# GpSimd stands until a landing behind every four indirect transfers in a row instead of every six

## The chip, the cores and the metric

The kernel runs on one core of a Trainium2 chip. The number that counts is the device time of one execution in microseconds (us), as the median of the runs shown. A profile is one separate execution with the hardware profiler on; it has its own span and its own time.

The engines are named as in the profile: PE (TensorE matmul), PEld (its weight loads), DVE (VectorE), ACT (ScalarE), POOL (GpSimd), SP (SyncE, which here only issues plain transfers). A name with a q, such as SPq, is the engine's instruction queue.

## The reference, cut to what matters

The input is 32 sequences of 128 tokens with 128 features. Two layers follow, each a conditioning step and a mixture of experts, and each adds its result to `x`:

```
x = x + moe_attention(modulated_head_mixing(x, cond))     # layer 0
x = x + moe_ffn(conditioned_embedding(x, ids, states))    # layer 1

# layer 0: 16 experts, softmax over the experts whose gate is open, at least the two best
q, k, v = (sum_e w[n, e] * (h[n] @ proj[e]) for each of the three projections)
o       = softmax(q k^T / sqrt(128)) v                    # per sequence
out[n]  = sum_e w[n, e] * (o[n] @ o_proj[e])
# layer 1: 8 experts, the two best, weights from their logits
out[n]  = sum_e c[n, e] * (silu(h[n] @ gate[e]) * (h[n] @ up[e])) @ down[e]
```

What counts here is that a token goes to two experts. So a token's row has to be carried to the place of its expert and its result carried back.

## The kernel before, in words

**The sparse path.** The function `two_experts` does the work. (A second function, `every_expert_kernel`, stands behind a branch for inputs in which some token needs more than two experts, and is not run with these inputs.) Tokens are taken in four parts of eight tiles of 128 tokens in each layer. For a part, `front0` or `front1` computes the conditioned rows and the gates, and `route` works out for each token and each of its two experts a row number (`place` for the way there, `back` for the way back). Rows are then moved through DRAM, sorted by expert into blocks of 128 rows.

**Six kinds of indirect transfers.** They move 128 rows each, they are all issued by POOL, and there are 64 of each kind, 384 in all (`scatter` and `gather`):

- `rows_x`: the rows of layer 0 to their experts (scatter), before the q, k, v projections
- `gq`: the q, k, v rows back to the tokens (gather, 384 features), before the attention of one tile
- `rows_o`: the attention's rows to their experts (scatter)
- `ygo`: the output projection's rows back (gather), added to `X`
- `rows_c`: the rows of layer 1 to their experts (scatter)
- `ygc`: the rows of layer 1 back (gather), added to `X`, which goes to `out` afterwards

Between them SP moves whole blocks with plain transfers: `crx`, `cro` and `crc` read the sorted rows, `outs_x`, `outs_o` and `outs_c` write the experts' results. A read of a part's blocks waits for all of its scatters, and a gather waits for all of its results. The experts' matmuls are `qkv` and `yo` in layer 0 and `gu` (gate and up) and `yc` (down) in layer 1. The gather buffers are few: four of `gq`, three pairs of `yg`.

**The planner.** The kernel is not written in the order in which it runs. Class `Turns` records every operation as a node, with the time that it is expected to take and its dependencies, and `arrange` makes an order for all engines at once: `backward` gives due times, `forward` is a list schedule that keeps a clock for each engine, and the best of `ROUNDS` passes is taken. `trace` then emits the instructions in that order, and each engine runs its own list strictly in it. Since one helper emits them all, nearly every row of the profile has line L341.

**The rests.** `forward` counts POOL's transfers in a row. A transfer continues the run if it can begin less than `GAP` (1.2 us by the planner's clock) after the one before it. When the run has reached `RUN`, the planner lets POOL's clock pass by `REST` (1.6 us) and notes a rest before that transfer:

```
if not node.size or begin - free[name] >= self.GAP:
    run = 0
elif run == self.RUN:
    begin, run = free[name] + max(self.REST, begin - free[name]), 0
    rests.add(i)
run += 1 if node.size else 0
```

In the program a rest is a memset of eight columns of a tile `idle` that nobody reads (line L620). `trace` gives it, and it alone, a real wait on the instructions before it in POOL's list; for an indirect transfer that is its landing. If the instructions before it are scatters of one group, it waits for all of them. What comes after the memset on POOL stands behind it.

Of the kernel before, what the change touches and what calls it, by code (L numbers as in the profile page):

```python
# [110 lines left out]
class Turns:  # L111
# [20 lines left out]
        "POOL": {"rows_x": 1.45, "rows_o": 1.32, "gq": 1.29, "rows_c": 1.25, "ygo": 1.23, "ygc": 1.22},  # L132
    }
    TABLES = {AF.Exp: "exp", AF.Tanh: "tanh", AF.Silu: "silu"}
    RUN, REST, GAP = 6, 1.6, 1.2
    LOOK, HASTE = 0.8, 10.0
    HOP = 0.05
    READ_US, WRITE_US, ROWS_US = 1.7, 1.9, 1.2
# [2436 lines left out]
```

## Time and profile before

| | before |
|---|---|
| runs | 916.92, 911.39, 911.41 us; median 911.41 us |
| profiled execution, its own time | 922.13 us |
| its span, first to last instruction | 920.2 us |
| mean granted TensorE clock | 0.812 |
| busy share: PE, PEld, DVE, ACT, POOL | 66%, 45%, 55%, 45%, 44% |
| POOL: indirect transfers, rests | 384, 58 |
| DMA moved | 116.39 MB, 126 GB/s over the span |
| share of 16 DMA engines: SP's transfers, POOL's transfers | 30.1%, 12.4% |

The profiled execution took 1.2% more than the median of the runs, so differences are carried over rather than absolute times. A group's row gives line, engine, operation, output and inputs, count, busy time, mean of one in ns, and after the second bar the engine's idle time just before such instructions with what ended most of it. The busy time of a transfer on POOL is that of issuing it; its landing is seen only in who waits for it.

### The profile page before, as it was taken

How to read it: one execution, taken by the hardware profiler on the slowest of the kernel's cores; microseconds unless marked ns; L12 is line 12 of the kernel's file. 1: busy time of each engine (PE TensorE's matmuls, PEld its weight loads, DVE VectorE, ACT ScalarE, POOL GpSimd, SP SyncE). 2: the span in 40 equal slices, each digit the busy share in tenths (PEclk: the TensorE clock that was granted, in tenths of full speed). 3: DMA queues.
4: the chain of work that ended last, by engine and by line, in shares of the span. 5: the costliest groups of instructions: out<-in, count | busy, mean ns of one | idle time of the engine just before them, and what ended most of it. 6: DMA issues, size and time to landing. Idle time of an engine off the chain costs nothing.

```text
span 920.2 us, 10753 instructions
## 1 busy us (share of the span) xinstructions
PE 610.7 (66%) x2962; PEld 412.7 (45%) x2962; DVE 509.9 (55%) x1629; ACT 410.1 (45%) x1076; POOL 406.8 (44%) x457
## 2 busy tenths in 40 slices
PE   5167456975875686383676556767787878898830
PEld 3155335553553555251544344435464545665520
DVE  7988989687896460020465636534724765532311
ACT  3223342643654464271474246465453454453420
POOL 1000044056366664454555555455556562554424
PEclk9577577996998799596877578679998999797975
DMA  7980003421625578569733273431545214124221
GB/s 202 319 246 1 0 29 90 172 101 50 198 80 172 163 215 273 163 199 293 198 93 81 64 193 97 105 107 46 145 138 145 55 61 120 47 73 136 76 66 48
DMA packets 134043, 116.39 MB, mean 126 GB/s; under 512 B 9560, under 2 KB 121112, under 8 KB 133976
## 3 DMA queue, kind: packets, MB, share of 16 engines
q1 hardware_dynamic: 119640, 82.04, 30.1%
q0 software_dynamic: 14336, 33.58, 12.4%
q8 instruction: 28, 0.46, 0.2%
q14 instruction: 39, 0.32, 0.1%
HBM read 56.86 MB, written 58.72 MB: 126 GB/s over the span
## 4 chain that ended last, share of the span: by engine, by line
PE 32%; DMA 16%; issue 12%; POOL 9%; ACT 6%; DVE 5%; another core or an unknown queue 2%; POOLq 0%; SPq 0%; ACTq 0%; DVEq 0%
PE gu L341 7%; PE yc L341 4%; DMA gq<-outs_x,back 4%; DMA outs_x<-yx 3%; DMA ygo<-outs_o,back 3%; POOL rows_x L341 3%; PE qkv L341 3%; PE phT L341 2%; DMA rows_x<-h,place 2%; POOL gq L341 2%; PE yo L341 2%; PE pre L341 2%; PE pat L341 2%; PE pcrc L341 1%
## 5 line engine op out<-in xcount | busy, mean ns | idle before, releaser
L341 POOL DMA_INDIRECT rows_x<-h,place x64 | 79.3, 1240 | 187.8 <-DVE place L341 130.4
L341 PE MATMUL pat<-ident,prodv 128*128 128x128 f32 x512 | 79.3, 315 | 38.9 <-DVE prodv L341 18.1
L341 PE MATMUL gu<-w1e,crTc 128*128 x176 | 97.1, 650 | 3.5 <-DVE hh L341 2.6
L341 PE MATMUL qkv<-wq,crTx 128*128 x216 | 86.7, 524 | 9.6 <-ACT yx L341 7.5
L341 POOL DMA_INDIRECT ygc<-outs_c,back x64 | 60.8, 950 | 71.5 <-DMA outs_c<-ycs 45.1
L341 PEld LDWEIGHTS pat<-ident,prodv 128*128 128x128 f32 x512 | 68.9, 164 | 48.6 <-issue 25.2
L341 POOL DMA_INDIRECT gq<-outs_x,back x64 | 69.0, 1078 | 28.1 <-issue 18.6
L341 DVE TENSOR_TENSOR prodv<-S,kx 128x2048 f32<-128x2048 f32 x32 | 72.9, 2289 | 11.7 <-PE pat L341 11.3
L341 POOL DMA_INDIRECT rows_o<-orow,place x64 | 66.0, 1031 | 22.8 <-issue 17.0
L341 DVE TENSOR_TENSOR hh<-hh,gu 128x256 f32<-128x256 f32 x88 | 36.7, 418 | 68.8 <-ACT hh L341 52.3
L341 POOL DMA_INDIRECT rows_c<-crow,place x64 | 62.2, 973 | 25.0 <-issue 19.6
L620 POOL MEMSET idle<- 128x8 f32 x58 | 6.1, 104 | 147.2 <-DMA ygo<-outs_o,back 35.1
L341 POOL DMA_INDIRECT ygo<-outs_o,back x64 | 60.9, 952 | 22.4 <-issue 17.5
L341 ACT COPY yx<-qkv 128x384 f32<-128x384 f32 x108 | 50.5, 482 | 27.9 <-PE qkv L341 12.0
L341 PE MATMUL yc<-w1e,hT 128*128 x352 | 54.4, 296 | 11.7 <-ACT ycs L341 5.8
L341 DVE SCALAR_TENSOR_TENSOR X<-ygc,share,X 128x128 f32<-128x128 f32 x64 | 21.3, 348 | 71.3 <-DMA ygc<-outs_c,back 51.4
L341 PEld LDWEIGHTS yc<-w1e,hT 128*128 128x128 f32 x352 | 48.2, 206 | 23.5 <-ACT hT L341 11.2
L341 DVE SCALAR_TENSOR_TENSOR gq<-gq,w 128x384 f32<-128x384 f32 x32 | 19.5, 615 | 68.9 <-DMA gq<-outs_x,back 57.3
L341 ACT ACTIVATE hh<-gu 128x256 f32<-128x256 f32 x88 | 34.5, 392 | 51.7 <-PE phT L341 33.3
L341 PEld LDWEIGHTS qkv<-wq,crTx 128*128 128x128 f32 x216 | 38.6, 202 | 33.6 <-ACT yx L341 13.4
L341 DVE SCALAR_TENSOR_TENSOR X<-ygo,w,X 128x128 f32<-128x128 f32 x64 | 21.8, 344 | 52.4 <-DMA ygo<-outs_o,back 47.4
L341 DVE TENSOR_TENSOR prod<-kx 128x1152 f32<-128x1152 f32 x32 | 43.3, 1353 | 4.9 <-issue 1.8
(289 smaller groups left out, 1404.9 us busy)
## 6 DMA issues: line engine op xcount, KB each, us to landing
outs_x<-yx SPq DMA_DIRECT2D x24, 768.0 KB
crx<-rows_x SPq DMA_DIRECT2D x12, 512.0 KB
cro<-rows_o SPq DMA_DIRECT2D x12, 512.0 KB
outs_o<-yos SPq DMA_DIRECT2D x12, 512.0 KB
crc<-rows_c SPq DMA_DIRECT2D x8, 512.0 KB
outs_c<-ycs SPq DMA_DIRECT2D x8, 512.0 KB
rows_x<-zeros SPq DMA_DIRECT2D x2, 1728.0 KB
rows_o<-zeros SPq DMA_DIRECT2D x2, 1728.0 KB
```

The source lines that it names most:

```text
L341: node.give = lambda: getattr(real, op)(turns.real(out), *map(turns.real, args), **{k: turns.real(v) for k, v in kw.items()})
L620: tn.rest = lambda: nc.gpsimd.memset(idle, 0.0)
```

## The change

One constant of the planner is changed. A rest is put in when the run has reached four transfers instead of six. The rest itself, the planner's price for it (`REST`) and the gap that ends a run (`GAP`) stay as they were. The order of all engines is planned anew with it.

```
-    RUN, REST, GAP = 6, 1.6, 1.2
+    RUN, REST, GAP = 4, 1.6, 1.2
```

## The prediction

> **What bounds the kernel now.** I read the page's groups first, then POOL's timeline, then the table by stage, then the chain. In the groups (busy, mean ns | idle before and its releaser) POOL's rests stand out: the memset itself is 104 ns, but POOL is idle before it.
>
> ```profile
> L620 POOL MEMSET idle<- 128x8 f32 x58 | 6.1, 104 | 147.2 <-DMA ygo<-outs_o,back 35.1
> L341 POOL DMA_INDIRECT gq<-outs_x,back x64 | 69.0, 1078 | 28.1 <-issue 18.6
> ```
>
> That is 147.2 / 58 = 2.54 us of standing per rest. POOL's timeline (start, us, what, idle before) shows one rest in place, and a transfer issued after a long pause:
>
> ```profile
> 315.42 0.95 POOL L341 DMA_INDIRECT rows_o<-orow,place  x1 [0.30 <-issue]
> 318.18 0.11 POOL L620 MEMSET idle<- 128x8 f32 x1 [1.81 <-DMA rows_o<-orow,place]
> 318.85 0.96 POOL L341 DMA_INDIRECT rows_o<-orow,place  x1 [0.56 <-issue]
> ...
> 257.83 1.80 POOL L341 DMA_INDIRECT rows_x<-h,place  x1 [11.61 <-DVE place L341]
> ```
>
> Without a rest the next transfer begins 0.30 us after the last one ends. With it, it began at 318.85 after an end at 316.37: 2.48 us, so the rest costs 2.48 - 0.30 = 2.18 us there. I worked this out for all 58: mean 2.94 us, least 1.77, most 6.41.
>
> The table by stage (us, then PE, PEld, DVE, ACT and POOL busy with counts, PE clock, DMA share, GB/s):
>
> ```profile
> 188.00:258.00 70.00, 48.98 (x252) 34.33 (x250) 57.16 (x105) 34.68 (x95) 37.47 (x33) 0.83 0.33 102
> 258.00:348.00 90.00, 65.37 (x331) 45.22 (x331) 59.57 (x145) 48.67 (x141) 60.26 (x55) 0.89 0.53 173
> 348.00:600.00 252.00, 153.88 (x718) 105.35 (x716) 96.86 (x467) 115.76 (x282) 130.04 (x153) 0.75 0.54 158
> 600.00:888.00 288.00, 232.80 (x1157) 152.46 (x1157) 133.47 (x580) 138.57 (x371) 140.62 (x166) 0.91 0.33 94
> 888.00:920.20 32.20, 0.00 (x0) 0.00 (x0) 5.62 (x16) 0.00 (x0) 15.31 (x18) 0.50 0.18 50
> ```
>
> POOL's 44% busy hides the truth of 188 to 600. There it issues 208 transfers (224.4 us of busy time), with 208 x 0.30 = 62 us between them and 32 rests of 3.26 us each (104 us). Together that is 391 of 412 us. Only three pauses are no rest: 11.6, 5.3 and 2.1 us, together 18 us above the usual 0.30. So in this stretch POOL works without a break, and what it carries is waited for: over the whole run DVE stands 57.3 us for `gq` and 47.4 us for `ygo`. From 600 on PE is busy 81% of the stage and sets the pace; behind 888 there are only `ygc` gathers and their additions.
>
> The chain of waits says the same (start, us, what):
>
> ```profile
> 572.03 5.87 DMA rows_c<-crow,place
> ...
> 578.21 0.10 POOL idle L620
> 578.32 0.56 issue
> 578.88 0.96 POOL rows_c L341
> ```
>
> Here a rest is a link of the chain: landing, memset, next scatter. Counting such links from 188 to 600 gives 14 of the 32 rests, with a mean cost of 3.24 us; from 600 to 888 none of 22; behind 888 both.
>
> **The change part by part.** I listed POOL's queue as each program builds it. Before: 384 transfers, 58 rests. After: 384 transfers, 90 rests. By the transfers they stand behind: the first 16 (`rows_x` of part 0) 2 to 3; the next 208, which are 188 to 600, 32 to 50; the next 144, to 888, 22 to 34; the last 16 (`ygc` of part 3) 2 to 3. No transfer is added or taken away. SP issues the same plain transfers with few places swapped, while about a fifth of DVE's and ACT's lists differ in order. I price that at nothing, within plus or minus 5 us as an estimate: no stage or dependency is altered by it.
>
> *First 16 scatters, one more rest.* POOL starts them when `place` is ready (122.0) and SP's queue stands for their landing (`crx` goes out at 153.35). Behind the added rest is the remainder of the part, and all of it is on the path. The two rests there cost 1.77 and 3.18, mean **2.5 us**.
>
> *188 to 600, 18 more rests.* What is queued behind an added memset is every later gather and scatter, and for those wait DVE (`gq`, `ygo`), PE (attention) and SP (`crx`, `cro`, `crc`). Two bounds. From below: the share of rests that is on the chain stays 14 of 32, so 18 x 14/32 = 7.9 rests at 3.24 = 25.5 us. From above: POOL is never caught up, so all 18 x 3.26 = 59 us arrive at 600, or 41 us if the 18 us of pauses take up part. I take 25.5, since it is counted on the path, and keep 41 and 59 for the range. The covers of the other rests are PE and DVE work on the front of the next parts; if that cover goes, the sum moves to the upper bound. At the floor of 1.77 per rest the lower figure would be 14 us.
>
> *600 to 888, 12 more rests.* None of 22 is on the chain. POOL pauses here anyway, waiting for `outs_c`: 16.5 us at 780, 7.6 at 843 and 21.0 at 888, 45 us in all against 12 x 2.59 = 31 us of added standing. Hidden behind PE: **0**. Without that cover it is 31. The thin spot is 832, where the last scatter of part 3 ends as the read `crc` goes out on the chain.
>
> *The last 16 gathers, one more rest.* Nothing else runs. The two rests cost 2.42 and 2.08, mean **2.25 us**.
>
> *Does a shorter run make anything cheaper?* The Trainium skill, DMA: Bandwidth & Descriptors, section on the anatomy of a SWDGE DMA, puts some 2.0 us of fixed cost on such a transfer, most of it the receipt of the last write. Taken as the price of one wait (plus 64 KB / 436 GB/s = 0.15), it makes the 7.9 rests 17 us and the whole 22. The row says 3.24 per rest: up to 6.41 where the landing meets SP's writes. I go by the row. The other hope is that issuing itself gets faster with fewer transfers in flight: 33 us of the 384 transfers' busy time lie above 0.95 us each. By place in the run the mean excess is 0.08, 0.12, 0.07, 0.06, 0.08, 0.12 us from first to sixth, with no trend, and the transfer at 257.83 took 1.80 us after 11.6 us of standing. The skill's SBUF page (SBUF: two separate sides) has another reason, that some DVE operations lock GpSimd out while it writes descriptors; by stage the row fits it: mean 1.27 us from 188 to 348 where DVE is busy 73%, 0.97 behind 348 where it is 38%. By depth, dropping the fifth and sixth place would save some 3 us; by the lock nothing. I take nothing.
>
> **Sum:** 2.5 + 25.5 + 0 + 2.25 = +30 us. The profiled execution, 922.1, would become 952. Carried to the median of the runs, 911.4 + 30 = **942 us**, 3.3% slower.
>
> **The rivals.** About 1% (9 us) is what a measurement of this kernel can tell from no change.
>
> *POOL alone is the bound (0.25).* All added rests up to 600 arrive at the hand-over to layer 1's experts, whose first blocks wait for `rows_c` of part 0 (last scatter at 583.9). For: the account of 391 of 412 us. Against: half the chain there is PE, DVE or SP. 41 + 4.75 = 46 gives 957; without the pauses 59 + 4.75 = 64 gives 975.
>
> *Only the ends pay (0.13).* The added rests in the middle fall where the chain is elsewhere, or the new order starts gathers early enough. For: 18 of 32 rests there were off the chain. Against: DVE's waits for gathers. 2.5 + 2.25 gives 916.
>
> *Less crowding pays (0.05), faster.* Fewer transfers of POOL in flight let late landings come early. The place: eight on the chain, `outs_x` 8.78 and 6.92 us against 4.4, `gq` 5.75, 6.73 and 5.77 against 3.6, `ygo` 5.60, 5.91 and 5.26 against 2.5. If all became ordinary: 6.9 + 7.5 + 9.3 = 24 us, less 4.75 gives 892. It decides only if nearly none of the 18 rests comes onto the chain; with 7.9 of them even at 1.77 us it is a wash. Against: SP's own transfers use 30.1% of the DMA engines, POOL's 12.4%, and the former stay.
>
> That the change does nothing is excluded by the queue: 90 against 58.
>
> **How the numbers follow.** The likeliest case has 0.57 and 930 to 957 as its own range (14 to 41 us in the middle). With the first two rivals' ends the range is 915 to 968: it takes in 916, and most of 957 to 975. Slower by over 1%: 0.57 + 0.25 = 0.82; within 1%: 0.13; faster: 0.05.
>
> **What would show it.** Right: 90 memsets on L620 with 200 to 265 us of idle before them; 2 to 4 us per rest between 188 and 600; more rests as links of the chain there; the last `ygc` stage 2 us longer; PE's busy time unchanged and its idle time grown mostly ahead of layer 1's experts; issue times by place in the run the same. Wrong: a mean standing well under 2 us (the runs of six were themselves the backlog), or the growth lying behind 600 (layer 1's scatters had no cover), or a changed order that shifts stages by more than 5 us where no rest is on the chain.

## The result, and the profile after

The changed kernel took 971.24 us (median of 4 runs, 969.3 to 974.57), the kernel before 913.76 us (median of 4: the three runs of the table above and one more). The ratio is **1.063 (95% interval 1.0575 to 1.0686)**: 57.5 us slower. The forecast was 30 us slower, 942 us, with a range of 915 to 968.

One plain fact has to come first. The experiments ran on four chips, called A (e1 to e4), B (e5 to e8), C (e9 to e12) and D (e13 to e18) below. On A and B stands appear while POOL sends long runs of transfers: ACT, and often DVE or PE, wait for something that the trace doesn't name. C and D show none. In this text such waits are given as the time in which at least one engine stands so, counted once where they overlap. The profile of before that the prediction read has 24 us of them, the profile after has none. So before was profiled once more, on chip D (e17: median 917.04 us, span of the profile 913.0), and that page is compared with after's here (span 967.5). Each experiment's ratio compares with before on the same chip; for the result itself the chips are not on record.

The groups after, in the form of the lines shown before (busy, mean ns | idle before and its releaser):

```profile
L620 POOL MEMSET idle<- 128x8 f32 x90 | 9.6, 106 | 206.6 <-DMA gq<-outs_x,back 53.8
L341 POOL DMA_INDIRECT gq<-outs_x,back x64 | 67.8, 1059 | 26.1 <-issue 16.9
L341 DVE SCALAR_TENSOR_TENSOR gq<-gq,w 128x384 f32<-128x384 f32 x32 | 19.7, 616 | 115.4 <-DMA gq<-outs_x,back 89.1
```

and the same in the second profile of before:

```profile
L620 POOL MEMSET idle<- 128x8 f32 x58 | 6.1, 105 | 148.0 <-DMA rows_o<-orow,place 32.9
L341 POOL DMA_INDIRECT gq<-outs_x,back x64 | 68.7, 1074 | 24.1 <-issue 17.4
L341 DVE SCALAR_TENSOR_TENSOR gq<-gq,w 128x384 f32<-128x384 f32 x32 | 19.5, 615 | 81.4 <-DMA gq<-outs_x,back 54.1
```

There are 90 rests for 58, and the idle time ahead of their memsets grew by 58.6 us. Issuing is as dear as it was: the 384 transfers are 397.9 us of busy time against 399.5. DVE's wait for `gq` landings rose from 54.1 to 89.1 us. POOL's timeline after shows a rest behind the fourth transfer, the end at 359.27 to the next start at 363.01, 3.74 us in place of the usual 0.30:

```profile
358.31 0.96 POOL L341 DMA_INDIRECT gq<-outs_x,back  x1 [0.30 <-issue]
362.23 0.10 POOL L620 MEMSET idle<- 128x8 f32 x1 [2.95 <-DMA gq<-outs_x,back]
363.01 1.24 POOL L341 DMA_INDIRECT rows_x<-h,place  x1 [0.68 <-issue]
```

The stages are cut where the 17th, the 225th and the 369th transfer go out. The table of after (us, then PE, PEld, DVE, ACT and POOL busy with counts, PE clock, DMA share, GB/s):

```profile
187.00:640.00 453.00, 275.50 (x1309) 188.04 (x1308) 217.40 (x732) 201.48 (x523) 228.04 (x259) 0.76 0.47 141
640.00:933.00 293.00, 225.96 (x1146) 149.09 (x1144) 129.88 (x558) 137.08 (x365) 141.84 (x177) 0.90 0.31 88
933.00:967.50 34.50, 0.00 (x0) 0.00 (x0) 5.62 (x16) 0.00 (x0) 15.47 (x19) 0.50 0.17 47
```

and of before, second profile:

```profile
187.00:602.00 415.00, 264.77 (x1304) 184.71 (x1302) 214.81 (x729) 199.38 (x522) 227.93 (x241) 0.79 0.51 153
602.00:880.00 278.00, 227.67 (x1149) 150.05 (x1149) 131.05 (x568) 137.48 (x367) 140.35 (x165) 0.91 0.33 93
880.00:913.00 33.00, 0.00 (x0) 0.00 (x0) 5.63 (x16) 0.00 (x0) 15.32 (x18) 0.50 0.19 49
```

The engines do nearly the same work in each row, and the stretch is longer. (PE's busy time in the middle stage grew by 10.7 us with 5 matmuls more, at a granted clock of 0.76 for 0.79.) The next table is from POOL's timelines, by the exact starts. Standing is what lies between two transfers with a rest, less the usual 0.30 us, so it holds the memset and the pauses on both sides of it:

| stage | longer by | rests | standing in rests | pauses |
|---|---|---|---|---|
| up to the 17th transfer | -0.1 | +1 | 3.7 to 6.4 (+2.7) | |
| 17th to 225th | **+38.0** | +18 | 110.9 to 155.5 (+44.6) | 17.3 to 12.4 (-4.9) |
| 225th to 369th | **+15.4** | +12 | 52.9 to 75.8 (+22.9) | 44.0 to 36.2 (-7.8) |
| from the 369th | +1.2 | +1 | 4.5 to 6.3 (+1.8) | |
| sum | +54.5 | +32 | +72.0 | |

Pauses are POOL's idle time at transfers without a rest, above 0.30 us each. In both long stages the growth is the added standing less what the pauses gave way, within 1.7 us (POOL's issuing became that much shorter in the second row). This is bookkeeping along POOL's list; that the standing is the cause is for the experiments to show. The chain view of after covers only its last 5 us and can't be used.

### The profile page after: what moved, and what is told of

Read it like the earlier page. It is cut to its first block, busy times and chain, and to the rows that moved or that the text cites. A ratio compares the mean times of both kernels' runs of the same rounds, so it can differ in the third digit from the quotient of the medians.

```text
span 967.5 us, 10808 instructions
## 1 busy us (share of the span) xinstructions
PE 609.2 (63%) x2962; PEld 411.2 (43%) x2962; DVE 511.4 (53%) x1629; ACT 410.9 (42%) x1076; POOL 409.9 (42%) x489
## 5 line engine op out<-in xcount | busy, mean ns | idle before, releaser
L341 POOL DMA_INDIRECT rows_x<-h,place x64 | 82.0, 1282 | 183.1 <-DVE place L341 125.8
L620 POOL MEMSET idle<- 128x8 f32 x90 | 9.6, 106 | 206.6 <-DMA gq<-outs_x,back 53.8
L341 DVE SCALAR_TENSOR_TENSOR gq<-gq,w 128x384 f32<-128x384 f32 x32 | 19.7, 616 | 115.4 <-DMA gq<-outs_x,back 89.1
L341 POOL DMA_INDIRECT rows_o<-orow,place x64 | 64.3, 1005 | 24.4 <-issue 17.3
L341 ACT ACTIVATE gq<-gq,w 128x384 f32<-128x384 f32 x32 | 19.7, 617 | 92.6 <-DMA gq<-outs_x,back 92.6
L341 PEld LDWEIGHTS qkv<-wq,crTx 128*128 128x128 f32 x216 | 40.9, 210 | 37.7 <-ACT yx L341 9.0
L341 PE MATMUL yc<-w1e,hT 128*128 x352 | 49.3, 282 | 1.8 <-ACT hT L341 1.0
L341 PEld LDWEIGHTS yc<-w1e,hT 128*128 128x128 f32 x352 | 45.1, 195 | 10.9 <-ACT hT L341 5.3
```

Source lines behind the costliest of these rows:

```text
L341: node.give = lambda: getattr(real, op)(turns.real(out), *map(turns.real, args), **{k: turns.real(v) for k, v in kw.items()})
L620: tn.rest = lambda: nc.gpsimd.memset(idle, 0.0)
```

## The experiments

Most kernels here use one edit that separates the two things that one constant does: `RUN` still makes the order, and `EMIT`, read by a small helper `rests_of`, decides in that order where a rest is emitted (a list of "from this transfer on, behind every so many"; 0 is none).

```
-    RUN, REST, GAP = 6, 1.6, 1.2
+    RUN, REST, GAP = 6, 1.6, 1.2; EMIT = [(0, 4)]
...
-        traced = []
+        traced, rests = [], rests_of(nodes, best[1], best[3], self.EMIT)
         for i in best[1]:
-            if i in best[3]:
+            if i in rests:
```

In the traces DVE, ACT, POOL and SP run through the same operations as before (or as after, where the new order is named), one by one in the same order; only the memsets differ.

### Waits or order? (chip A, before 929.25 us)

e1: the old order with a rest behind every four, `RUN` 6 and `EMIT = [(0, 4)]`.

> The order of all engines is that of the kernel before; only rests are put in behind every four transfers (88 instead of 58). Theory A (the added landing waits act in series on POOL, the order is of no matter): as slow as the changed kernel within 1.5%, so a ratio to before of 1.05 to 1.075. Rival B (the new order of PE, DVE, ACT and POOL is what costs): within 1.5% of before. Both halves: about 1.03.

Measured: 987.82 us, ratio 1.062 (1.056 to 1.069), with 88 rests. So the added rests alone lose as much as the whole change. Per added rest it is 58.6 / 30 = 1.95 us. Two things limit this. The changed kernel was not run on chip A, so the equal ratios come from different chips. And on a chip with stands, rests of four also keep the stands away (5.7 us of them in e1, 24 us in the first profile of before), so the 58.6 us are what is left after that gain.

e2: the new order with a rest behind every six, `RUN` 4 and `EMIT = [(0, 6)]`.

> The order of the changed kernel, planned for runs of four; rests are emitted only behind every six (60 of them). Theory A: back at before, ratio 0.99 to 1.015. Rival B: it stays at 1.05 to 1.07.

Measured: 912.26 us, ratio 0.981 (0.976 to 0.987), with 60 rests. So the changed order alone is no loss; here it is a gain of 17 us.

e4: the old order, `EMIT = [(0, 6), (16, 4), (224, 6)]`: rests of four in the middle stage alone.

> The order of before; rests behind every four only from the 17th to the 224th transfer, behind every six elsewhere (75 rests, 17 more than before). The prediction's step (only the share of rests seen on the chain, 14 of 32, counts) gives +25 us, ratio 1.027. Theory A (in that stretch every added rest of some 3 us arrives, less the pauses) gives +37 to +45 us, ratio 1.04 to 1.05.

Measured: 967.65 us, ratio 1.043 (1.038 to 1.048), with 75 rests: 38.4 us for 17 rests, 2.26 each.

e3: the old order without any rest, `EMIT = [(0, 0)]`.

> The order of before, with no rest at all (58 taken out). Theory A: POOL gets 104 us back between the 16th and the 224th transfer; other engines become the bound before all of it is saved, so 4 to 8% faster than before (ratio 0.92 to 0.96). Rival C (a rest protects from something: with more transfers in flight issuing slows down or landings come late): ratio 0.99 or more, and the issue of a transfer takes clearly more than 0.96 us late in a long run.

Measured: 983.13 us, ratio 1.058 (1.053 to 1.063), slower than with 58 rests. ACT's timeline in layer 1's experts shows how:

```profile
663.06 0.37 ACT L341 COPY ycs<-yc 128x256 f32<-128x256 f32 x1 [6.12 <-remote]
666.61 0.38 ACT L341 ACTIVATE hh<-gu 128x256 f32<-128x256 f32 x1 [3.18 <-remote]
666.89 0.37 ACT L341 COPY hT<-phT 128x256 f32<-128x256 f32 x1
673.75 0.38 ACT L341 ACTIVATE hh<-gu 128x256 f32<-128x256 f32 x1 [6.50 <-remote]
674.03 0.37 ACT L341 COPY hT<-phT 128x256 f32<-128x256 f32 x1
680.78 0.38 ACT L341 ACTIVATE hh<-gu 128x256 f32<-128x256 f32 x1 [6.38 <-remote]
```

Between pieces of 0.4 us ACT stands 6 us, and the releaser is "remote": no recorded event explains it. DVE stands with it (its `hh` at 674.17 after 6.37 us of idle), and so does PE, whose next matmuls need `hT`. POOL meanwhile sends `rows_c` without a break:

```profile
672.79 0.96 POOL L341 DMA_INDIRECT rows_c<-crow,place  x1 [0.30 <-issue]
674.05 0.96 POOL L341 DMA_INDIRECT rows_c<-crow,place  x1 [0.30 <-issue]
675.31 0.96 POOL L341 DMA_INDIRECT rows_c<-crow,place  x1 [0.30 <-issue]
```

Such waits take 168 us here, 32 in e2, 5.7 in e1 (rests of four). In e2 there are thirteen, and twelve of them reach into the sixth transfer of a run or the rest behind it. At this point it looked as if rests of six were a balance: fewer rests, more stands. That held on chip A; see below.

### The late stage, shorter pauses, five in a row (chip B, before 926.5 us)

e5: the old order, `EMIT = [(0, 6), (224, 4), (368, 6)]`.

> The order of before; a rest behind every four transfers only from transfer 225 to 368 (the stage behind 600 us), elsewhere behind every six: 11 more rests. The prediction priced this stage at 0 (PE hides it): a ratio of 0.995 to 1.005. The theory that every added rest delays POOL's whole list, and that the cover was not there: the whole-kernel run with rests of four stood 20 us above the one with the middle alone, of which the first and last stage have 4 to 5, so about +15 us, a ratio of 1.012 to 1.02.

Measured: 944.17 us, ratio 1.018 (1.012 to 1.024): 17.7 us for 11 rests, 1.6 each. The stage that the prediction priced at 0 pays. With e4's 38.4 the two make 56.1 us, and e1, which has both and the ends, lost 58.6: the stages add up, as far as two chips can be compared.

e6: before's order and its 58 rests, but the memset no longer waits for a landing and is long instead.

```
-RESTING = 8
+RESTING = 2048
...
-  mybir.DependencyClass.Sync if node.give == self.rest else mybir.DependencyClass.NoSync,
+  mybir.DependencyClass.NoSync,
```

> The order of before, its 58 rests in their places, but none waits for a landing: the memset writes 2048 columns of idle instead of 8 and lasts about 2.1 us (by the 768 columns in 0.81 us of before), so POOL leaves a gap of nearly the same length. If it is the pause that protects the other engines: the time of before, 0.98 to 1.01, and waits with no recorded releaser of some 20 us in all as before. If it is the landing itself (nothing in flight when the next run begins): slower, towards the 1.058 of no rest at all, with 100 to 200 us of such waits.

Measured: 896.95 us, ratio 0.969 (0.962 to 0.976), with 41 us of unexplained waits. A pause of 1.82 us without a landing keeps most of the stands away (e7, without rests on this chip, has 139 us), and POOL stands 1.70 us per rest (1.82 + 0.18 - 0.30) instead of 2.97. A landing is not what a rest is for on this chip.

e7: the new order without rests.

> The changed kernel's order with no rest at all. Theory: long unbroken runs hold up all engines in any order, so 0.982 of the new order with rests of six plus what the old order lost, 1.03 to 1.05 of before, with some 200 us of waits with no recorded releaser. Rival: the loss without rests belonged to the old order, which was planned with them; then the new one runs without them at 0.95 to 0.98.

Measured: 991.84 us, ratio 1.073 (1.066 to 1.080), with 139 us of unexplained waits. The stands don't belong to one order.

e8: the new order, `EMIT = [(0, 5)]`.

> The changed kernel's order with a rest behind every five transfers. If the time goes by the number of rests alone, it lies between the order's 0.981 with six and the changed kernel's 1.063 with four: about 1.01 to 1.03, 2.4 us per rest more than with six. If the held-up engines at the sixth place of a run are worth as much as the rests (all but one of them in the run with six were there), five is as good as six or better: 0.97 to 0.985.

Measured: 934.83 us, ratio 1.013 (1.008 to 1.018), 75 rests. In this order the time goes with the number of rests: with 60 it had 0.981 on chip A, with 90 the change had 1.063. The three figures come from different chips.

### How much of POOL's standing arrives (chip C, before 916.21 us)

e9: the changed kernel with e6's edit, 90 long memsets and no landing.

> The changed kernel, its 90 rests in their places, but the memset writes 2048 columns (1.8 us) and waits for no landing. A rest then costs POOL 1.7 us instead of 2.71, 91 us of standing less in all. Theory (the lost time is POOL's standing, whatever makes it stand): of before's 72 us less standing without landings 29 us arrived, of the added rests' 73 us some 57; so 36 to 71 us less than the changed kernel, 0.99 to 1.025 of before. Rival (the extra landings themselves cost, the pause is free): 0.95 to 0.97, the same as with six pauses without landings.

Measured: 889.53 us, ratio 0.971 (0.966 to 0.976). The standing fell from 244.1 us to 158.0 in the trace (90 x 1.70 = 153 by the pauses alone) and the ratio by 0.092, 84 us: more than expected, nearly all of the 86.

e10: the new order, `EMIT = [(0, 6)]`, with e6's edit.

> The changed kernel's order, a rest behind every six, of 2048 columns and with no wait for a landing. If the new order's gain (0.981) and the pause's (0.969) add up: 0.945 to 0.96. If both are the same gain (POOL less late): 0.965 to 0.98.

Measured: 861.05 us, ratio 0.939 (0.935 to 0.944), a little better than the two gains together (0.981 x 0.969 = 0.951, both from other chips). Against e9, on the same chip and in the same order, 30 pauses more cost 28.5 us, though none waits for a landing. So POOL's standing costs time whatever makes it stand; a landing costs more at least because it lasts longer (2.71 us against 1.70).

e12: e6 with `RESTING = 1024`. e11: e6 with `RESTING = 8`, a bare memset of 0.13 us.

> As the run with 2048 columns and no landing, with 1024 columns: a memset of about 0.95 us, a rest costs some 0.8 us instead of 1.7. If the protection goes with the length of the pause: between no rest (1.058) and the whole pause (0.969), 1.0 to 1.03. If a short pause is enough: 58 x 0.9 = 52 us less standing, of which 0.4 arrives: 0.945 to 0.955.

> The order of before, its 58 memsets of 8 columns in their places, but without the wait: POOL leaves about 0.4 us instead of 0.3. If the pause's length protects, this is a kernel with no rest: 1.04 to 1.06, with 150 to 200 us of waits with no recorded releaser. If any other instruction between transfers is enough: 0.93 to 0.96.

Measured: e12 832.10 us, ratio 0.910 (0.904 to 0.915); e11 812.97 us, ratio **0.888** (0.883 to 0.894). Neither has an unexplained wait. On this chip nothing has to be kept away, or a memset of 0.13 us does it: e3 and e11, 17% apart in ratio, differ in 58 such memsets and in the chip. e13 and e14 tell these apart.

### The memset or the chip? (chip D, before 916.1 us)

> The same kernel as in the earlier run with no rest (1.058), now beside the one with bare memsets, on one chip. If the memset of 0.1 us itself protects the other engines: again 1.05 to 1.07, with whole-core stands of 4 to 8 us while POOL sends an unbroken run. If the stands came with the chip of that batch: 0.88 to 0.90, as the bare memsets did on another chip, and the bare memsets as well wherever this chip has none.

> The same kernel as in the earlier run with 58 bare memsets (0.888), beside the one with none. If the memset protects: 0.88 to 0.90 again on this chip, with the kernel with none at 1.05 or more. If the chip decides: both within 0.02 of each other.

Measured: without any rest (the very kernel of e3) 816.01 us, ratio **0.888** (0.884 to 0.893); with 58 bare memsets 813.41 us, ratio 0.887 (0.881 to 0.893). It was not the memsets but the chip, or what else differed between the two occasions: each chip had its own time, so chip and hour can't be told apart. ACT passes the same six instructions in e13 without a stand, 3.5 us from first to last where e3 took 17.7, again while POOL is in an unbroken run (25 transfers from 575.24 on):

```profile
578.66 0.37 ACT L341 COPY ycs<-yc 128x256 f32<-128x256 f32 x1 [0.21 <-PE yc L341]
579.96 0.39 ACT L341 ACTIVATE hh<-gu 128x256 f32<-128x256 f32 x1 [0.92 <-DVE l0mv L341]
580.24 0.37 ACT L341 COPY hT<-phT 128x256 f32<-128x256 f32 x1
581.04 0.39 ACT L341 ACTIVATE hh<-gu 128x256 f32<-128x256 f32 x1 [0.43 <-PE phT L341]
581.32 0.37 ACT L341 COPY hT<-phT 128x256 f32<-128x256 f32 x1
582.12 0.39 ACT L341 ACTIVATE hh<-gu 128x256 f32<-128x256 f32 x1 [0.43 <-PE phT L341]
```

e16: the old order with a bare memset behind every 24, 12 in all.

> The order of before with a bare memset only behind every 24 transfers in a row, 12 in all. If the memset ends what builds up behind some six transfers: most of the stands are back, 1.0 to 1.05. If the kernel does not need the memsets at all: 0.88 to 0.89, the same as with 58.

Measured: 816.34 us, ratio 0.892 (0.889 to 0.896). The memsets are not needed here.

e15: the changed kernel with its 90 memsets bare.

> The changed kernel with its 90 memsets in their places and no wait for a landing. If all that the change costs is POOL's standing: 90 x 2.7 us of standing go, and the time is that of before's order with 58 bare memsets, 0.87 to 0.90 (0.02 less if the new order is the better one here as well). If a part of the cost lies in the order or in the memsets: above 0.91.

Measured: 826.46 us, ratio 0.900 (0.897 to 0.904). Without the landing waits the changed kernel is 10% faster than before. It is still 13 us behind e14: the order planned for rests of four is the worse one once nobody rests. On chip A it was the better one by 17 us. So what the order is worth depends on the rests that are then emitted, or on the chip, and that stays open.

e17: the kernel before, once more. e18: the bare memsets, once more.

> The kernel before, unchanged, for a profile of it on the chip of this batch. On a chip without whole-core stands: no wait without a recorded releaser (the first profile had 21 us of them), 58 rests of 2.9 us, and the middle stage (188 to 600 before) shorter by up to 10 us. On a chip with stands: some 20 to 30 us of them, all at the sixth place of a run.

> 58 bare memsets, no landing wait, for a third chip. On a chip where before shows stands: if a memset of 0.1 us ends what builds up in a run, 0.88 to 0.92; if only a pause or a landing does, 1.04 to 1.07, like no rest at all on the first chips. On a chip without stands: 0.885 to 0.89 once more, and the question stays open.

Measured: e17 917.04 us, ratio 1.000 (0.997 to 1.003), no unexplained wait; its middle stage was 415.2 us against 416.3 in the first profile, so the 7 us by which this profile is shorter lie mostly in the late stage (278.1 against 283.1). e18 815.03 us, ratio 0.890 (0.885 to 0.896). It was chip D again; whether bare memsets help on a chip like A or B was not seen.

Put in order of POOL's standing, the kernels without stands make a curve (the standing is the sum in each trace; some of it, 12 us in e11 and up to 43 in e15, is waiting for data at a place where a rest stands):

| kernel | order | POOL's standing at rests, us | ratio to before |
|---|---|---|---|
| e11, bare memsets (chip C) | old | 12 | 0.888 |
| e12, half pause (chip C) | old | 54 | 0.910 |
| before | old | 172 | 1.000 |
| e15, bare memsets (chip D) | new | 43 | 0.900 |
| e10, pauses behind six (chip C) | new | 112 | 0.939 |
| e9, pauses behind four (chip C) | new | 158 | 0.971 |
| changed (chip not on record) | new | 244 | 1.063 |

In the old order, of the first 42 us of added standing some 19 us arrive (0.45 of them), of the next 118 some 84 us (0.71). In the new order it is 0.52, then 0.63, and of the last 86 us nearly all. In either order, the more POOL stands, the more of the next rest is paid.

## Why the prediction was wrong, point by point

- **The direction and the mechanism were right.** POOL's added standing for landings is the cost. With the old order and more rests there is a loss of the same size (e1), with the changed kernel's rests in place but no landing waits it is gone (e9, e15).
- **The step that failed is the 14 of 32** in the middle stage: the share of the rests that were links of the chain was taken as the share of added standing that arrives. The terms were 18 rests at 3.24 us and 0.44 of that, 25.5 us. Measured: 18 rests added 44.6 us (2.48 each), and 38.0 us arrived, 0.85 of it; e4, in the old order, lost 38.4 us by 17 rests in this stage. The price was put too high, the share far too low. A chain follows one path. A rest off that path still delays every later transfer of POOL, and the prediction's own account (391 of 412 us busy, between and resting) left only 18 us to take that up; 4.9 us of the 17.3 in the second profile did. The rival with POOL as the bound and the pauses taken off, 41 us, is this stage to 3 us. Chance 0.25 was too little for it, but its total of 957 was too low as well, for it too had the late stage at 0.
- **600 to 888 at nothing failed too**, as the prediction's own sign of being wrong has it (growth behind 600). Measured: +15.4 us of the 22.9 added, and 17.7 us in e5. The cover was to be the three waits for `outs_c`. After has them as before, only the first is shorter. POOL's timeline of the second profile of before, then of after:

```profile
778.10 0.97 POOL L341 DMA_INDIRECT ygc<-outs_c,back  x1 [15.32 <-DMA outs_c<-ycs]
880.23 0.94 POOL L341 DMA_INDIRECT ygc<-outs_c,back  x1 [18.56 <-DMA outs_c<-ycs]
```

```profile
824.24 0.98 POOL L341 DMA_INDIRECT ygc<-outs_c,back  x1 [10.16 <-DMA outs_c<-ycs]
933.52 0.94 POOL L341 DMA_INDIRECT ygc<-outs_c,back  x1 [17.82 <-DMA outs_c<-ycs]
```

  The last wait keeps 17.82 of its 18.56 us. What it waits for comes out of experts whose rows POOL scattered. By these dependencies a later scatter moves the wait and doesn't fill it; no run here tests this reading by itself. "None of 22 on the chain" came from one profile; in the second one of the same kernel a late rest is a link of it (chain, then POOL's timeline at the same place):

```profile
669.67 0.96 POOL rows_c L341
670.62 3.99 issue
...
675.39 0.97 POOL rows_c L341
```

```profile
674.73 0.10 POOL L620 MEMSET idle<- 128x8 f32 x1 [4.10 <-DMA rows_c<-crow,place]
```

- **The ends.** The last 16 gathers: 1.8 us of added standing and 1.2 us of stage against 2.25. The first 16: 2.7 us were added, but the first scatter went out 2.0 us sooner (119.47 against 121.46), so the read `crx` behind them went out only 0.6 us later (153.49 against 152.86), against 2.5. In the sum of the profiles 2.5 + 25.5 + 0 + 2.25 became -0.1 + 38.0 + 15.4 + 1.2 = 54.5 us.
- **The order at 0, plus or minus 5 us**, was too narrow: -17 us with rests of six (e2), +13 us with none to wait for (e15 against e14). What it was worth with rests of four is not known: e1 and the changed kernel have the same ratio, but on different chips, and the profile of e1 is 22 us longer than that of the changed kernel (989.9 against 967.5).
- **Issuing unchanged** was right (397.9 against 399.5 us).
- **Less crowding pays** was rightly put low for fast landings. The rests do protect something, which the prediction had not seen, but on two of four chips only, and in part: with rests of six 32 us of such waits remain in e2.
- The mean standing by the page's 2.0 us of fixed cost (the Trainium skill, DMA: Bandwidth & Descriptors, on the anatomy of a SWDGE DMA) would have been too low: a rest is 2.71 us in the profile after. From the start of the last transfer to the memset that waits for its landing it is 3.31 us there on average, and 2.36 at least.

## What to carry to other kernels

Where an in-order engine is issuing or waiting for its own landings nearly the whole stage, price an added wait at its full length less the pauses that don't depend on that engine: the share of such waits on the chain is no marginal price, and a pause that the same queue's earlier work brings about is no cover. Before shortening the runs between two waits, take the waits out once and see what they buy, on more than one chip: without landing waits or pauses this kernel is 11% faster than before on two chips (on C with bare memsets, on D also with none) and 6 to 7% slower on two others (without memsets; bare ones were not run there). Long memsets without a landing behind every six ran on a chip with stands and on one without, and were faster on both (0.969 in the old order on chip B, 0.939 in the new one on chip C).

## What the runs showed of the hardware

- The same kernel without rests has the ratio 1.058 on chip A and 0.888 on chip D. On A and B, ACT, and often DVE or PE with it, stands for up to 18 us at a time while POOL sends long runs of indirect transfers; the trace names no releaser (168 us in e3, none in e13). Whether the chip, something beside it at that hour, or the recording of the profile makes the difference, no run shows.
- Short runs keep the stands away: 168 us without rests, 32 with runs of six (new order) and 5.7 with runs of four (old order), all on chip A.
- Rests beside SP's traffic are the long ones. In the second profile of before, a rest is 3.74 us on average where SP issued a plain transfer between 4 us before the run's last transfer and 1 us behind its start (29 rests), and 2.19 us at the other 29. In the profile after it is 3.49 (38 rests) and 2.14 us (52).
- PE's busy time and its clock go with POOL's standing: the same 2962 matmuls took 575.7 us at a granted clock of 0.843 in e13, 600.8 at 0.811 in the second profile of before, 609.2 at 0.797 after. How much of the change's loss comes by way of the clock was not separated.
